# Two transfers at an image boundary: the fourth pair's spread reciprocals are issued two steps later

## The chip, the cores and the metric

The kernel runs on one core of a Trainium2 chip. The metric is the time of one execution in microseconds on the device; the lower the better. The core has five engines that run their own instruction streams: PE (matmuls; its weight loads are shown as PEld), DVE (vector), ACT (activations, casts; it also issues transfers), POOL (vector) and SP (issues most transfers). Each stream is in order. Engines and transfers wait for each other through counters (semaphores).

## The reference, cut to what matters

Two layers over a batch of 8 images of 384 channels and 32 x 32 = 1024 positions. The change lies in layer 0, an attention over the positions of one image with 8 heads of 48 channels and a relative bias:

```python
qkv = (tokens @ qkv_w + qkv_b).reshape(b, n, 3, NUM_HEADS, HEAD_DIM)
attn = jnp.einsum('bhnd,bhmd->bhnm', q * scale, k)
attn = attn + _relative_bias(h, w, mlp_w1, mlp_b1, mlp_w2, mlp_b2)[None]
attn = jax.nn.softmax(attn, axis=-1)
out = jnp.einsum('bhnm,bhmd->bhnd', attn, v)
out = out @ proj_w + proj_b
```

with `x + out` as its result, group norm ahead of it. Layer 1 is a second attention with 6 heads and a feed-forward part with quantised activations. All is float32.

## The kernel before, in words

Layer 0 goes image by image (`b` = 0 to 7). The 8 heads are held as four pairs (`pair` 0 to 3; the two heads of a pair, `j`, take 64 partitions each). The first three pairs carry 48 channels of their own and 16 channels of the fourth pair beside them; the fourth pair (`NF0` = 3) is put together from those by transfers between partitions.

*Units.* Per image there are 16 batches of four score units. `run` computes the scores of a batch (L920, tiles `s`), DVE adds the bias (L927), ACT takes the exponential (L931), and one batch later PE multiplies by `v` (L893). The row of ones in `v` gives the softmax sums, so `oT` holds the outputs not yet divided, and the sums beside them.

*Dividing.* When a pair is done, `divide` (named `divide` in the listing below) brings its sums to DRAM (L956) and back in another shape (L960), POOL takes reciprocals (L961), they go to DRAM (L967, `keep_inverse`), are loaded spread over 64 partitions for each of the two heads (L984, `spread`, tile `rb`, two loads of 256 KB), and POOL multiplies (L988, `multiply`). For the fourth pair `spread_rows` (L1000, `oT<-oT`, six transfers of 64 KB) then copies its rows to beside the first three pairs, because the output projection (`products`, L1011, tiles `pp`) reads three tiles with all 64 rows of both heads in use. `project_out` of image `b` is run inside image `b + 1`, after its first batch. It adds `res`, the image itself, loaded by SP (L1021).

*Between two images.* The next image's q and k are computed between its predecessor's last batch and its own first one, in six blocks (`BLOCKS0`; block 1 is the keys of pair 0, block 2 its queries, 3 the keys of pair 1, 4 its queries, 5 the keys of pair 2, 6 its queries). A block is three groups of products on PE (L171, `pm` and `pg`), one instruction on ACT (L677) and one on DVE (L683, `take` and `add`), and then `halves`: a cast on ACT to the high part (L696), a subtraction on DVE for the low part (L697), and transfers of both to DRAM: the high part is issued by ACT, the low one by SP (`halves<-h`, `halves<-t`; L701 is the whole tile of 512 KB, L703 two pieces of 64 KB). After block 3, PE computes `v` in four parts (`project_v`, L776). After v's second part `fill_q` and after the third `fill_k` issue the transfers that complete the first pair's queries and keys on chip (L719: `h<-t`, `km<-h`, `km<-l`, `h<-l`, `l<-h`, two each, ten in all, called fills here). Blocks 4 to 6 follow; then the new image's first batch, which reads the filled tiles, then `pp` of the old image, then the second batch.

*What sets the order.* A framework writes the waits. Beside it, the kernel puts off work by steps: `later.after(n, work)` runs `work` at the n-th `later.step()` from there. Between images, each block's `add` and each part of `v` is one step: blocks 1 to 3 are steps 1 to 3 after the last batch's `divide`, v's four parts are 4 to 7, blocks 4 to 6 are 8 to 10. A work's step sets its place in the streams of SP and POOL. The tuple `at` in `divide` holds such numbers: `at[0]` for `keep_inverse`, `at[1]` for `spread`, and from there `at[2]` for `multiply` and, for the fourth pair, from there `at[3]` for `spread_rows`.

*Transfer counters.* The framework gives the transfers of SP and ACT eight counters in turn, in the order in which it places them, and a transfer waits until the one that used its counter before has landed. Which two transfers are paired so is seen in the built program, not in the source.

The last image and the first three pairs take other branches of the same `if`.

Of the kernel before, what the change touches and what calls it, by code (L numbers as in the profile page):

```python
# [275 lines left out]
def _layer0(tc, ins, x1, sums, shared, weights, beside):  # L276
# [9 lines left out]
    with ExitStack() as ctx:  # L286
# [40 lines left out]
        for g in range(P // QT):  # L327
            at = g * QN
# [516 lines left out]
        def weigh(b, u, es):  # L845

            pair, h, m2 = u
            if m2 == 0:
                acc[b, pair] = mm2(f"o{b}_{pair}_{h}")
            po = acc[b, pair]  # L850
            for i in range(2):
                for r in range(2):
                    keys = ts(r, QP)
                    for j in range(2):
                        nc.tensor.matmul(  # L855
                            po[ts(j, S0), r], v[keys, 2 * m2 + i, 2 * pair + j, :],
                            es[j][keys, ts(i, HALF)], start=(m2 == 0 and i == 0),
                            stop=(m2 == MT // 2 - 1 and i == 1),
                        )
            if m2 < MT // 2 - 1:  # L860
                return None
            o = oT[:, pair, ts(h, HALF)]
            nc.scalar.copy(o, po[:, 0])

            def finish():
                nc.vector.tensor_add(o, po[:, 1], o)
                if h == NH - 1:
                    divide(b, pair)

            return finish  # L870
# [8 lines left out]
        class Batches:  # L879
# [7 lines left out]
            def weigh(self):  # L887
                pair, h, g, es = self.held
                self.held = None
                po = mm2(f"o{self.b}_{pair}_{h}_{g}")[:, 0]  # L890
                for i in range(BT):
                    for j in range(2):
                        nc.tensor.matmul(  # L893
                            po[ts(j, S0)], v[:, BT * g + i, 2 * pair + j, :],
                            es[i][:, ts(j, HALF)], start=(i == 0), stop=(i == BT - 1),
                        )

                def finish():
                    o = oT[:, pair, ts(h, HALF)]
                    if g == 0:  # L900
                        nc.scalar.copy(o, po)
                        return
                    nc.vector.tensor_add(o, po, o)  # L903
                    if h == NH - 1:
                        divide(self.b, pair)

                return finish
# [39 lines left out]
        def divide(b, pair):  # L947


            o = oT[:, pair]  # L950
            sd = dram.tile([2, N], F32, tag="sd", name=f"sd{b}_{pair}")
            rd = dram.tile([2, N], F32, tag="rd", name=f"rd{b}_{pair}")
            mine = sums[:, b, pair]
            inv = kept.tile([P, 2 * N // P], F32, tag="inv", name=f"inv{b}_{pair}", bufs=2)
            for j in range(2):
                nc.sync.dma_start(sd[j : j + 1], oT[j * S0 : j * S0 + 1, pair])  # L956

            def invert():
                with nc.allow_non_contiguous_dma(reason="sums"):
                    nc.sync.dma_start(mine, sd.rearrange("j (p c) -> (j p) c", c=2 * N // P))  # L960
                    nc.gpsimd.tensor_tensor(  # L961
                        inv, mine, over.to_broadcast([P, 2 * N // P]), ALU.pow
                    )

            def keep_inverse():
                with nc.allow_non_contiguous_dma(reason="sums"):
                    nc.sync.dma_start(rd.rearrange("j (p c) -> (j p) c", c=2 * N // P), inv)  # L967

            if b == B - 1 or b == 0 and pair < NF0:
                invert()  # L970
                at = (2, 2 if pair == NF0 else 3, 2, 0)
            elif pair == NF0:
                invert()
                at = 2, 5, 2, 1
            else:
                later.after(1, invert)
                at = 3, 4, 2, 0
            later.after(at[0], keep_inverse)
            rb = []

            def spread():
                rb.append(kept.tile([P, N], F32, tag="rb", name=f"rb{b}_{pair}"))
                for j in range(2):
                    nc.sync.dma_start(rb[0][ts(j, S0)], rd[j].partition_broadcast(S0))  # L984
                later.after(at[2], multiply)

            def multiply():
                nc.gpsimd.tensor_mul(o, o, rb[0])  # L988
                if b == B - 1:
                    if pair < NF0:  # L990
                        for j in range(2):
                            nc.gpsimd.memset(oT[j * S0 : j * S0 + SP, pair], 0.0)
                elif pair == NF0:
                    later.after(at[3], spread_rows)

            def spread_rows():
                for c in range(NF0):
                    for j in range(2):
                        row = j * S0 + SP + c * FR
                        nc.sync.dma_start(oT[j * S0 : j * S0 + SP, c], oT[row : row + FR, pair])  # L1000

            later.after(at[1], spread)
# [70 lines left out]
        for i in range(len(parts) // 2):  # L1073
            later.after(i + (13 if i < 9 else 12), lambda: grow_turns(1))
            at = 1 + i % NF0 if i < 12 else 2 + i % 2
# [1502 lines left out]
```

## Time and profile before

| | us |
|---|---|
| median of three runs | 2915.94 (2912.86 to 2917.39) |
| the profiled execution | 2915.22 |
| its span | 2913.4 |
| PE busy | 2872.4 (99%) |
| DVE busy | 2010.5 (69%) |
| ACT busy | 1554.4 (53%) |
| POOL busy | 492.7 (17%) |

Layer 0 takes the first 1340 us; the boundaries between its images lie 160 us apart, the first at about 230 us. In a line of the timeline or of the chain the first number is the start from the span's begin, the second the duration, then engine, line, operation and `output<-inputs`; an engine's name with q is its queue issuing a transfer. In brackets is the idle time of the engine ahead of the instruction, and what ended it. Times of landing are those of a transfer's last counter event in the trace. The windows view gives, for a stretch, the busy time of PE, PEld, DVE, ACT and POOL with the number of instructions, the granted clock of PE as a share of full speed, and the use of the transfer engines.

### The profile page before, as it was taken

Reading aid. Unit: us, or ns where it says so; the run is one execution under the profiler, and the core shown is the slowest. Engines: PE = TensorE matmul, PEld = TensorE weight load, DVE = VectorE, ACT = ScalarE, POOL = GpSimd, SP = SyncE. Lnnn points to the kernel's source line nnn. Section 1 sums busy time; section 2 is a strip of 40 time slices with the busy share of each in tenths; the row PEclk is TensorE's granted clock in tenths of the full one; section 3 lists DMA queues with packets and bytes.
Section 4 is the critical chain, followed back from the end, with each engine's and each line's share of the span. In section 5 each row is a group of like instructions: output and inputs, shape, how many; then the busy total and the mean of one; then the engine's idle time right before and its main releaser. Section 6 shows DMA issues by size and latency. Waiting matters only on the chain.

```text
span 2913.4 us, 43519 instructions
## 1 busy us (share of the span) xinstructions
PE 2872.4 (99%) x16850; PEld 1648.2 (57%) x16850; DVE 2010.5 (69%) x2041; ACT 1554.4 (53%) x1888; POOL 492.7 (17%) x318
## 2 busy tenths in 40 slices
PE   8999999999999999999999999999999999999998
PEld 3465564646464554644546647647647647655553
DVE  3886868686777768673756865865865875865756
ACT  2655636364555647362734655555555555564644
POOL 3120302121120202022102203203202202211010
PEclk9999999999999999999999999999999999999999
DMA  6657575665746474753301212112112112112111
GB/s 193 198 166 207 136 237 136 192 173 167 193 139 194 131 233 99 225 142 109 110 24 31 84 32 73 68 32 72 68 32 72 68 32 73 68 41 84 41 46 39
DMA packets 177751, 324.78 MB, mean 111 GB/s; under 512 B 75744, under 2 KB 94672, under 8 KB 176256
## 3 DMA queue, kind: packets, MB, share of 16 engines
q1 hardware_dynamic: 167552, 299.88, 36.1%
q10 hardware_dynamic: 9984, 22.02, 2.4%
q8 instruction: 137, 2.24, 0.3%
q14 instruction: 78, 0.64, 0.1%
HBM read 227.50 MB, written 80.65 MB: 106 GB/s over the span
## 4 chain that ended last, share of the span: by engine, by line
PE 86%; DMA 4%; DVE 4%; ACT 2%; issue 1%; SPq 1%; ACTq 0%; POOL 0%; DVEq 0%
PE o L893 14%; PE s L1930 11%; PE o L1979 11%; PE s L920 11%; PE y2p L2224 6%; PE pg L171 6%; PE y1p L2173 5%; PE pv L1867 4%; PE pm L171 3%; PE pp L2076 3%; PE pp L1011 3%; PE vg L776 2%; PE pq L1719 2%; PE s L824 1%; PE o L855 1%
## 5 line engine op out<-in xcount | busy, mean ns | idle before, releaser
L931 ACT ACTIVATE e<-e 128x1024 f32<-128x1024 f32 x448 | 473.9, 1058 | 324.9 <-DVE e L927 301.1
L927 DVE TENSOR_TENSOR e<-s,grow 128x1024 f32<-128x1024 f32 x448 | 517.4, 1215 | 86.6 <-PE s L920 79.8
L1941 ACT ACTIVATE e<-s,kc 128x512 f32<-128x512 f32 x768 | 464.0, 694 | 172.9 <-PE s L1930 163.3
L1930 PE MATMUL s<-qk,qk 64*64 64x512 f32 x3072 | 418.9, 592 | 1.7 <-DVE oT L1989 1.4
L1979 PE MATMUL o<-e,v 64*64 64x512 f32 x3072 | 414.5, 590 | 0.0
L893 PE MATMUL o<-e,v 128*64 128x512 f32 x1792 | 407.7, 598 | 1.3 <-DVE e L927 1.2
L1930 PEld LDWEIGHTS s<-qk,qk 64*64 64x64 f32 x3072 | 153.9, 132 | 191.9 <-issue 109.3
L1956 DVE TENSOR_TENSOR t<-t,e 128x1024 f32<-128x1024 f32 x192 | 230.9, 1221 | 45.2 <-ACT e L1941 45.0
L1979 PEld LDWEIGHTS o<-e,v 64*64 64x64 f32 x3072 | 160.6, 133 | 168.2 <-issue 141.1
L920 PE MATMUL s<-q,k 64*128 64x512 f32 x2016 | 254.0, 397 | 0.3 <-DVE oT L903 0.2
L893 PEld LDWEIGHTS o<-e,v 128*64 128x64 f32 x1792 | 120.5, 136 | 233.5 <-issue 217.2
L920 PEld LDWEIGHTS s<-q,k 64*128 64x128 f32 x2016 | 182.7, 184 | 104.2 <-DVE e L927 25.1
L961 POOL TENSOR_TENSOR inv<-sums,over 128x16 f32<-128x16 f32 x32 | 93.2, 2913 | 728.5 <-DMA sums<-sd 562.6
L2160 DVE TENSOR_REDUCE parts<-y 128x1 f32<-128x1024 f32 x75 | 89.7, 1217 | 103.2 <-ACT y L2157 102.7
L1953 DVE TENSOR_TENSOR t<-e,e 128x1024 f32<-128x1024 f32 x96 | 114.1, 1223 | 58.8 <-ACT e L1941 58.6
L1836 POOL TENSOR_TENSOR hc<-hc,rsqrt 128x32 f32<-128x32 f32 x24 | 137.9, 5747 | 2.0
L988 POOL TENSOR_TENSOR oT<-oT,rb 128x1024 f32<-128x1024 f32 x32 | 76.7, 2396 | 316.9 <-DMA rb<-rd 233.0
L1867 PE MATMUL pv<-wv,bx 128*128 128x384 f32 x384 | 128.3, 491 | 0.0
L2076 PE MATMUL pp<-oT,L_attn_proj_wT 128*128 128x512 f32 x288 | 126.3, 595 | 2.0 <-DVE oT L2042 2.0
L1011 PE MATMUL pp<-oT,wp 128*128 128x512 f32 x288 | 126.3, 596 | 1.0 <-issue 0.8
L1867 PEld LDWEIGHTS pv<-wv,bx 128*128 128x128 f32 x384 | 119.4, 314 | 9.8 <-ACT e L1941 4.1
L2173 PE MATMUL y1p<-lun,w 128*128 128x512 f32 x360 | 113.6, 396 | 2.8 <-DVE lun L2123 2.7
(242 smaller groups left out, 4256.2 us busy)
## 6 DMA issues: line engine op xcount, KB each, us to landing
rb<-rd SPq DMA_DIRECT2D x110, 256.0 KB
wc<-cut SPq DMA_DIRECT2D x42, 576.0 KB
k<-halves SPq DMA_DIRECT2D x84, 192.0 KB
wc<-there SPq DMA_DIRECT2D x25, 576.0 KB
halves<-h ACTq DMA_DIRECT2D x28, 512.0 KB
halves<-t SPq DMA_DIRECT2D x28, 512.0 KB
xn<-in_x_dram SPq DMA_DIRECT2D x24, 512.0 KB
res<-in_x_dram SPq DMA_DIRECT2D x24, 512.0 KB
```

What stands on the lines that cost most here:

```text
L171: self.nc.tensor.matmul(out[:, h], w[:, i, k], part[k][:, ts(h, HALF)], start=(k == 0 and i != 1), stop=(k == KC - 1 and i != 0),)
L893: nc.tensor.matmul(po[ts(j, S0)], v[:, BT * g + i, 2 * pair + j, :], es[i][:, ts(j, HALF)], start=(i == 0), stop=(i == BT - 1),)
L920: nc.tensor.matmul(ss[i][:, j], k[c][ts(j, S0), ts(BT * g + i, P)], q[a][ts(j, S0)], start=(m == 0), stop=(m == 2),)
L927: nc.vector.tensor_add(e.rearrange("p (j q) -> p j q", j=2), ss[i], near(2 * pair, BT * g + i, h, [GW * IW, 2]),)
L931: nc.scalar.activation(e, e, AF.Exp)
L1011: nc.tensor.matmul(pps[b, m][:, h], (wp[:, k] if k < NF0 else wl)[:, ts(m, P)], oT[:, k, ts(h, HALF)], start=(k == 0), stop=(k == (NF0 if ...
L1867: nc.tensor.matmul(pv[:, i, 0:C], xt[:, k].rearrange("c (p m) -> c m p", m=MT)[:, 2 * m2 + i], wv[:, k], start=(k == 0), stop=(k == KC - 1),)
L1930: nc.tensor.matmul(s[j][ts(c, QP), i], qk[pair, 1][rows, ts(4 * m2 + 2 * i + c, QP)], qk[pair, 0][rows, ts(h, HALF)], start=True, stop=True,)
L1941: nc.scalar.activation(e[:, ts(i, HALF)], s[j][:, i], AF.Exp, scale=kc[:, pair, j, m : m + 1])
L1956: nc.vector.tensor_add(total[j], total[j], e)
L1979: nc.tensor.matmul(po[ts(j, D1), r], v[keys, 2 * m2 + i, at : at + D1], es[j][keys, ts(i, HALF)], start=(m2 == 0 and i == 0), stop=(m2 == ...
L2173: nc.tensor.matmul(py[m][:, h], w1[:, k, ts(m, P)], un[k][i][:, ts(h, HALF)], start=(k == 0 and i == 0), stop=(k == KC - 1 and i == 1),)
```

## The change

For the fourth pair of every image but the last (`pair == NF0`, `b < B - 1`) `spread` is run at step 7 in place of 5, `multiply` one step later in place of two, and `spread_rows` one step after it as before. `keep_inverse` stays at step 2. In SP's stream the two `rb` loads move from ahead of the ten fills to behind them, and block 4's three `halves<-t` come ahead of the six `oT<-oT`. In POOL's stream the order of the instructions is the same. The matmuls and their order are the same.

```diff
             elif pair == NF0:
                 invert()
-                at = 2, 5, 2, 1
+                at = 2, 7, 1, 1
             else:
                 later.after(1, invert)
                 at = 3, 4, 2, 0
```

## The prediction

> **What bounds the kernel now.** I read the page first, then the waits of PE, then the chain at an image boundary, SP's queue there, and the windows view for the clock. The page says that PE is busy all the time, so only what takes time from PE counts.
>
> ```profile
> PE 2872.4 (99%) x16850; PEld 1648.2 (57%) x16850; DVE 2010.5 (69%) x2041; ACT 1554.4 (53%) x1888; POOL 492.7 (17%) x318
> ```
>
> PE's waits, longest in total first (engine, line, what it waited for: total, times, longest):
>
> ```profile
> PE s L920 <- DMA l<-h: 10.3, 6, 1.8
> ...
> PE s L920 <- DMA oT<-oT: 1.7, 1, 1.7
> ```
>
> The largest is at the seven boundaries between images of layer 0: the first scores of the new image wait for the last fill, `l<-h` (L719). The chain at the second boundary (start, us, what) shows why:
>
> ```profile
> 388.66 1.06 ACT h L696
> 389.72 0.02 issue
> 389.74 2.69 DMA halves<-h
> 392.43 0.02 issue
> 392.44 2.24 DMA l<-h
> 394.68 0.04 issue
> 394.73 4.37 PE s L920 x21
> 399.09 15.65 PE pp L1011 x36
> ```
>
> The fill is not late for its data: it is issued when ACT's copy `halves<-h` has landed. The built program hands out eight transfer counters in turn, and a transfer waits for the one that had its counter before; the built before pairs the last `l<-h` with ACT's copy of block 4. SP's queue at the same place:
>
> ```profile
> 377.06 1.26 SPq L984 DMA_DIRECT2D rb<-rd  x2
> 378.42 1.17 SPq L719 DMA_DIRECT2D h<-t  x2
> ...
> 385.21 7.74 SPq L719 DMA_DIRECT2D l<-h  x2
> 393.05 5.60 SPq L1000 DMA_DIRECT2D oT<-oT  x6
> 398.75 0.52 SPq L701 DMA_DIRECT2D halves<-t  x1
> ```
>
> The windows view (last fields: granted clock, DMA share, GB/s), second and third boundary:
>
> ```profile
> 386.00:419.00 33.00, 31.29 (x120) 17.62 (x120) 17.33 (x15) 10.58 (x11) 0.29 (x1) 0.95 0.72 222
> 549.00:581.00 32.00, 30.05 (x120) 16.37 (x120) 17.67 (x15) 10.40 (x10) 0.00 (x0) 1.00 0.73 217
> ```
>
> A clock of 0.95 over 33 us is 1.65 us lost, that is 3.3 us at half speed; the trace has it as 3.4 us at 0.5. It happens at boundaries 2, 4 and 6, right after the stall, and nowhere else before the last instructions. PE starts a pair of score products every 0.43 us there, against 0.23 us in later batches.
>
> **The change part by part.**
>
> *Work.* No instruction is added or removed; the two `rb` loads (256 KB each), the POOL multiply and six `oT<-oT` move. Per image SP issues the ten fills first, then `rb`, then block 4's three `halves<-t`, then `oT<-oT`.
>
> *The fills.* In before, `rb` lies ahead of them in the transfers: in the trace's landing events `rb` lands at 382.70 and 383.72 and the first fills at 384.0. In the built after each fill is paired with an earlier transfer of SP, ACT's copy of block 3 or the weights, all landed by 381. Issued one after the other at 0.6 us (1.17 us for two), with two waits of about 2.2 us (`l<-h`'s 2.24), the last lands at about 385. PE needs it at 392.3, so this stall goes at all seven boundaries, with 7 us to spare.
>
> *`rb` and the multiply.* `rb` is issued at about 383.4. Before, two loads took 377.06 to 383.72 in a full queue; so it lands between 387 and 390. The multiply (2.41 us, 383.88 before) ends by 389.8 to 392.4. Nothing else on POOL waits for it; only `oT<-oT` does.
>
> *What is late next.* The projection `pp` (L1011) needs `oT<-oT`: the first two for its first matmul. In after the first `oT<-oT` has the counter of ACT's big copy of block 5 (`halves<-h`, L701); in before it had block 4's, and only the fifth waited for block 5's. So `pp` now hangs on this chain of ACT:
> - cast of block 4 (L696): before at 388.66, waiting for PE. Its buffer is now one that the fills free, so it starts when ACT's L677 ends, 385.39 + 1.12 = 386.5: 2.13 us earlier.
> - its three copies, issued in 1.6 us, the last landing 2.53 us after its issue (393.13 before): 391.0 + d, where d is what contention adds.
> - cast of block 5, which waits for them: 393.20 before, 391.07 + d after. PE and DVE feed it by 390.7.
> - its big copy: 1.07 + 2.69 us (the row above, undisturbed): 394.83 + d.
> - two `oT<-oT`: 0.6 us to the second issue, 2.41 us to its landing (393.63 to 396.04 before), 0.1 us of hand-overs: `pp` at 397.9 + d, that is 4.73 us + d after the start that the cast of block 5 had in before.
>
> In before `pp` started 4.70, 5.82, 4.75, 5.89, 4.65, 5.43 and 4.64 us after that cast at the seven boundaries; at 5 and 6 it then waited 0.71 and 0.44 us more for `oT<-oT` (its matmuls at 886.60 and 1047.32), which the new spacing avoids. The gains before d are -0.03, 1.09, 0.02, 1.16, 0.63, 1.14 and -0.09: 3.9 us. Boundaries 1 and 7 further lose about 0.35 us each in before, where the second batch waits for `res` (landing 252.15, PE's next stage at 254.77); `res` is issued about 1 us earlier in after, so 0.7 us more: 4.6 us.
>
> *d.* Now SP's `halves<-t` of block 4 (512 KB, issued at about 388.9) runs beside ACT's copies. Bounds: 0 (the 2.53 us, alone), and 3.0 us: ACT's copies of block 3, issued at 371.77 and 372.40 beside SP's loads, landed at 376.51 and 377.88, 5.5 us for the last. Nearer is ACT's copy at 395.16 beside `oT<-oT`, 3.42 us, d = 0.9; but only the end of ACT's transfer meets SP's here, so I take d = 0.3. 7 x 0.3 = 2.1: the gain is 2.5 us.
>
> [...]
>
> *The clock.* Without the stall PE goes through the four score units at 0.23 us a pair, up to the fourth, which waits for DVE's first addition (1.23 us after L697's 1.23 us after the cast of block 5): it ends at about 395.7 + d. Then PE waits for `pp`, until 397.9 + d: 2.2 us idle, as long as the 2.1 us that it waits in before (392.6 to 394.73). In before three of seven such gaps were followed by 3.4 us at half clock. In `pp`, where one matmul follows another at 0.43 us, that costs 3.4 x 0.5 = 1.7 us. Bounds: none of seven (0) and all (11.9 us). I take three, as before: 5.1 us. What the gate cost in before is already in the gains of boundaries 2, 4 and 6.
>
> [...]
>
> *Sum.* -2.5 + 5.1 = +2.6 us, 0.09%. The profiled execution took 2915.22 us (span 2913.4), 0.72 below the median 2915.94. On the median: 2918.5 us.
>
> **The rivals.** What a measurement can tell from no change is about 0.2%, 5.8 us.
>
> *A: `pp` does not wait (faster).* If `oT<-oT` landed by the time PE reaches `pp`, the gain would be the stall and the slow clock: `pp` at about 395.9 instead of 399.0 at even boundaries, at 558.4 instead of 560.4 at odd ones: 3 x 3.1 + 4 x 2.0 = 17 us, 2899. For: `rb` and the multiply are early enough. Against: the counter of ACT's copy of block 5, which cannot land before 394.8. It decides if that copy were 1.9 us faster, which no row shows. Half of it, with no slow clock, would be 2907.
>
> *B: the slow clock falls into `pp` at most boundaries (slower).* Place: `pp` on PE. Price 1.7 us each. From five of seven on the loss passes 5.8 us (5 x 1.7 - 2.5 = 6.0); at seven 9.4, 2925. For: the gap is slightly longer, and a short wait of about 0.5 us before the fourth unit precedes it. Against: three of seven in before.
>
> *C: the change does not do what it says.* The fills stay behind a late transfer: no change, 2916. The pairing in the built after speaks against it.
>
> **How the numbers follow.** My case and all between 4.6 us faster (d = 0, no slow clock) and 5.8 slower: 0.56. A and what lies towards it: 0.12. B, or d near 1: 0.30. C: 0.02. So faster 0.12, same 0.58, slower 0.30. Range: the low end 2910 is the 4.6 us gain and a little of A; the high end 2926 is B with seven of seven; a tenth is left out on each side.
>
> **What would show it.** Right: no wait of PE for `l<-h`; `rb` behind the fills in SP's queue; ACT's cast of block 4 about 2 us earlier; PE waiting 1.5 to 2.5 us for `oT<-oT` ahead of `pp` seven times; windows at the boundaries with a clock under 1 at two to four places, now in `pp`. Wrong: `pp` following the scores without a wait (A); the clock under 1 at five or more, or not at all; ACT's copies of block 4 landing over 3 us after their issue (d too small).

## The result, and the profile after

The changed kernel takes 2937.38 us (median of four runs, 2933.4 to 2940.08) against 2916.66 us before (four runs, 2912.86 to 2918.36): the ratio is 1.0075, with a 95% interval of 1.0063 to 1.0087. It is 20.7 us slower. The prediction was 2918.5 us, range 2910 to 2926: the measured time lies outside, on the side of rival B. All four runs of the changed kernel have a granted clock of 0.993 over the span (the profiled run before: 0.998), so the half clock told of below is not that of one execution alone.

The page of the profile after (span 2933.8 us), engines' busy time:

```profile
PE 2878.7 (98%) x16850; PEld 1649.3 (56%) x16850; DVE 2010.2 (69%) x2041; ACT 1553.3 (53%) x1888; POOL 497.0 (17%) x318
```

PE has the same instructions and is busy 6.3 us longer; the other 14 us of the longer span (20.4) are idle time. Its two largest waits (what it waited for: total, times, longest) are at the image boundaries, and the wait for `l<-h` is gone, as it should be:

```profile
PE pp L1011 <- DVE e L927: 17.2, 7, 2.5
PE s L920 <- DVE e L927: 11.0, 7, 2.1
```

Before, the stall was 1.7 us at each of the seven boundaries, 12.0 us in all (the view puts the 1.7 us of the fourth down to `oT<-oT`). So 12.0 us of waiting went and 28.2 us came, at the same seven places. The first of the two lines is the wait ahead of `pp`, the second the wait ahead of the fourth score unit of the first batch, which PE starts when DVE has added the bias to the first. The group of `pp`'s products (busy us, mean ns of one | idle before) shows the third loss, in after and, behind it, in before:

```profile
L1011 PE MATMUL pp<-oT,wp 128*128 128x512 f32 x288 | 139.6, 647 | 17.2 <-DVE e L927 17.2
```

```profile
L1011 PE MATMUL pp<-oT,wp 128*128 128x512 f32 x288 | 126.3, 596 | 1.0 <-issue 0.8
```

The same 288 products take 13.3 us longer: PE's clock. (PE's whole busy time grows by less, because the first batch's scores, into which the half clock fell before, are shorter now: at the second boundary one pair of products follows another every 0.23 us where it was 0.43.) The windows view of after (last fields: granted clock, share of the transfer engines, GB/s), three of the seven boundaries:

```profile
386.00:421.00 35.00, 30.93 (x110) 17.59 (x110) 15.31 (x13) 9.38 (x9) 2.40 (x1) 0.95 0.74 218
550.00:587.00 37.00, 32.71 (x113) 18.56 (x113) 15.00 (x13) 9.70 (x10) 2.40 (x1) 0.91 0.75 218
714.00:752.00 38.00, 34.05 (x123) 20.21 (x123) 16.68 (x16) 10.49 (x10) 2.41 (x1) 0.96 0.76 216
```

Before, three of seven boundaries had a clock under 1; now all seven do. In the trace's clock record that is 34.1 us at half speed around the boundaries instead of 10.2.

From a boundary's first score to the end of the last product of `pp` it is 153.2 us in seven boundaries before and 175.4 after. Of the 22.1 us more, 9.0 lie ahead of `pp`'s first product and 13.1 within `pp`; about 1.7 us come back elsewhere (the span grew by 20.4). The chain at the second boundary (start, us, what) shows how `pp` becomes late:

```profile
389.30 1.04 ACT h L696
...
391.21 4.34 DMA halves<-h
...
395.65 1.06 ACT h L696
396.71 0.02 issue
396.74 1.23 DVE t L697
397.96 1.14 DVE e L927
399.10 1.13 DVE t L683
400.23 0.06 DVE e L927
400.29 0.99 issue
401.27 1.23 DVE e L927
402.50 0.04 issue
402.55 17.37 PE pp L1011 x36
```

The last of ACT's copies of block 4 takes 4.34 us from issue to landing (before: 2.53), so the cast of block 5 starts 6.36 us after that of block 4 (before: 4.54, 393.20 less 388.66), and with it everything that follows. ACT's stream before, at the same place:

```profile
390.12 1.24 ACTq L703 DMA_DIRECT2D halves<-h  x2
...
393.20 1.04 ACT L696 CAST h<-t 128x1024 fp32r<-128x1024 f32 x1 [0.62 <-DMA halves<-h]
```

The last steps of the chain after are a trap: the view puts `pp`'s wait down to DVE's addition L927, since it ended last (402.49). But the second `oT<-oT` landed at 402.41, and at all seven boundaries `pp` begins 0.14 to 0.25 us after that landing. Experiment e5 decides it. SP's queue at that place, and what it waited for:

```profile
387.05 1.22 SPq L719 DMA_DIRECT2D l<-h  x2
388.32 1.23 SPq L984 DMA_DIRECT2D rb<-rd  x2
391.61 0.34 SPq L701 DMA_DIRECT2D halves<-t  x1
392.00 2.10 SPq L703 DMA_DIRECT2D halves<-t  x2
399.49 3.71 SPq L1000 DMA_DIRECT2D oT<-oT  x6
```

```profile
SPq L1000 <- DMA halves<-h: 5.3, 1, 5.3
```

The multiply ended at 395.56, yet `oT<-oT` was issued at 399.49, 0.06 us after ACT's big copy of block 5 landed (399.43), whose counter it has; SP had nothing else to issue in between. At the other six boundaries it is 0.06 to 0.08 us. Right beside ACT's copies of block 4 (issued 390.36 to 391.21) SP now has `rb` (landing 393.00) and `halves<-t` (issued 391.61, landing 395.72).

### The profile page after: what moved, and what is told of

Read it like the earlier page. It is cut to its first block, busy times and chain, and to the rows that moved or that the text cites. A ratio compares the mean times of both kernels' runs of the same rounds, so it can differ in the third digit from the quotient of the medians.

```text
span 2933.8 us, 43516 instructions
## 1 busy us (share of the span) xinstructions
PE 2878.7 (98%) x16850; PEld 1649.3 (56%) x16850; DVE 2010.2 (69%) x2041; ACT 1553.3 (53%) x1888; POOL 497.0 (17%) x318
## 4 chain that ended last, share of the span: by engine, by line
PE 86%; DVE 5%; DMA 4%; ACT 3%; issue 2%; SPq 0%; ACTq 0%; POOL 0%; DVEq 0%
PE o L893 13%; PE s L1930 11%; PE o L1979 11%; PE s L920 10%; PE y2p L2224 6%; PE pp L1011 5%; PE y1p L2173 5%; PE pg L171 4%; PE pv L1867 4%; PE pp L2076 3%; PE pm L171 3%; PE s L824 2%; PE o L855 2%; PE pq L1719 2%; PE vg L776 1%
## 5 line engine op out<-in xcount | busy, mean ns | idle before, releaser
L927 DVE TENSOR_TENSOR e<-s,grow 128x1024 f32<-128x1024 f32 x448 | 517.6, 1216 | 87.7 <-PE s L920 82.9
L1930 PEld LDWEIGHTS s<-qk,qk 64*64 64x64 f32 x3072 | 153.9, 132 | 190.6 <-issue 109.8
L1011 PE MATMUL pp<-oT,wp 128*128 128x512 f32 x288 | 139.6, 647 | 17.2 <-DVE e L927 17.2
```

The lines of the kernel that those rows point to most:

```text
L927: nc.vector.tensor_add(e.rearrange("p (j q) -> p j q", j=2), ss[i], near(2 * pair, BT * g + i, h, [GW * IW, 2]),)
L1011: nc.tensor.matmul(pps[b, m][:, h], (wp[:, k] if k < NF0 else wl)[:, ts(m, P)], oT[:, k, ts(h, HALF)], start=(k == 0), stop=(k == (NF0 if ...
L1930: nc.tensor.matmul(s[j][ts(c, QP), i], qk[pair, 1][rows, ts(4 * m2 + 2 * i + c, QP)], qk[pair, 0][rows, ts(h, HALF)], start=True, stop=True,)
```

## The experiments

Three theories were set against each other. **P** (place): the counter of ACT's copy of block 5 holds `oT<-oT` back and makes `pp` late. **T** (transfers): SP's transfers beside ACT's copies of block 4 delay the cast of block 5. **G** (gate): PE's clock is halved after the gaps (34.1 us of it in after), and that is a loss of its own. X stands for the start of the cast of block 5. The cuts of e1 and e2 are against before, that of e6 is against e2 (also called rb_only), those of e3, e4 and e5 (after_pool) are against after, and that of e7 (pool_late) is against e5.

**e1, only the later half of the change**

```diff
-                at = 2, 5, 2, 1
+                at = 2, 5, 3, 1
```

> Only the later half of the change: rb is loaded ahead of the fills as before, but the multiply and the six oT<-oT come a step later, so that they stand behind block 4's halves<-t and carry the counter of ACT's copy of block 5. Before 2916.7 us, after 2937.4 us. Theory P (the place of oT<-oT makes the projection late): pp starts 6.9 us after the cast of block 5 (as after) instead of 4.6 to 5.8 (before), 12 us in seven boundaries, the wait for l<-h stays, and the half clock follows into pp at most boundaries (up to 13 us more): 2929 to 2941 us. Theory T (rb's transfers beside ACT's copies of block 4 are what costs): without them the copies land in 2.5 us again and the cast of block 5 is where it was: at most 2922 us. Theory G (the clock gate is most of the loss): whatever the place, the time follows the number of windows at half clock, 1.7 to 3.4 us each; with three of them the time stays under 2930 us.

Measured: 2950.66 us, ratio 1.0106 (1.009 to 1.0123). The chain at the second boundary:

```profile
396.72 2.51 DMA halves<-h
...
399.30 1.05 ACT h L696
400.35 0.02 issue
400.37 4.77 DMA halves<-h
405.14 0.02 issue
405.16 2.26 DMA oT<-oT
407.42 0.14 issue
407.55 18.39 PE pp L1011 x36
```

ACT's copies of block 4 take 2.5 us again, so T's part is absent, and still it is the slowest of these variants of `at`: P holds, beyond the range that was given for it. Here the second `oT<-oT` has the counter of block 5's copy, which now runs beside block 4's `halves<-t` and takes 4.77 us, so `pp` comes 8.2 us after X instead of 6.9. All seven boundaries have the half clock, 51.2 us in all.

**e2, only the first half of the change**

```diff
-                at = 2, 5, 2, 1
+                at = 2, 7, 0, 1
...
-                later.after(at[2], multiply)
+                if at[2]:
+                    later.after(at[2], multiply)
+                else:
+                    multiply()
```

> Only the first half of the change: rb is loaded behind the fills, the multiply is issued in the same step, and oT<-oT keep the step that they had before, ahead of block 4's halves<-t and with counters of landed fills. Theory P: pp no longer waits, it starts about 0.8 us after the last scores (about 4.7 us after the cast of block 5 instead of 6.9), 15 us less than after, and without that gap no half clock in pp, 13 us less: about 2909 us, faster than before. Theory T: rb still runs beside ACT's copies of block 4, which take 3.4 to 4.6 us, and the fourth score unit still waits 2 to 2.7 us for DVE: 2918 to 2930 us. Theory G: the gap ahead of the fourth score unit is as long as the one of before, which was followed by the half clock three times in seven: 5 us on top, about 2914 us.

Measured: 2916.27 us against 2917.5 before, ratio 0.9999 (0.9989 to 1.0009): no difference. Waits of PE, and of SP at the second boundary:

```profile
PE s L920 <- DVE res L1030: 6.1, 9, 1.1
PE pp L1014 <- DMA oT<-oT: 4.1, 5, 1.2
```

```profile
SPq L703 <- DMA halves<-h: 6.1, 1, 6.1
```

Moving `rb` alone costs nothing: the 20 us of the change come with the order of `oT<-oT` and block 4's `halves<-t` (P). That order is behind T too. Here `rb` still runs beside ACT's copies of block 4, but `halves<-t` come later, and the copies land 2.4 to 3.3 us after the last issue, not the 3.4 to 4.6 that T had for `rb`; the distance of the two casts is 1.8 us above that of the prediction's chain (4.57 us) in seven boundaries, where after has 12.2. `pp` starts 4.7 to 5.6 us after X, and no boundary is followed by the half clock. But the removed wait for `l<-h` brings nothing either. SP now waits 6.1 us for ACT's copy of block 6, by another such pair of counters, ahead of block 5's parts and `res`; the second batch's scores then wait for `res`. Theory P's 2909 us had left out that next wait.

**e3, PE kept busy while it waits for `oT<-oT`** (after, with three products more, which the first real product overwrites)

```diff
                 pps[b, m] = mm2(f"pp{b}_{m}")
+                if m == 0 and pairs[0] == 0 and b < B - 1:
+                    for _ in range(3):
+                        nc.tensor.matmul(
+                            pps[b, 0][:, 0, :C], wp[:, 0, :P], wp[:, 1], start=True, stop=True
+                        )
```

> The kernel after with three more matmuls (128 x 384, own weights, about 1.9 us together) into pp's accumulator ahead of its first product, which overwrites them. PE is then busy in most of the 3.0 us in which it waits for oT<-oT; pp's start doesn't move. Theory G: the half clock at the boundaries goes or gets rarer, and pp takes 14.7 us again instead of 16.2 to 17.8: 8 to 13 us less than after, 2924 to 2929 us. Theory P and T without the clock: the loss is the late start alone, and nothing is gained: 2937 us. If it is the gap ahead of the fourth score unit that sets the gate, the windows stay too.

Measured: 2929.29 us, ratio 1.0037 (1.0026 to 1.0047). That is 8 us less than after by the medians and 11 by the two ratios, and PE has more to do. The chain at the second boundary, and the group of `pp`'s real products:

```profile
394.77 1.06 ACT h L696
...
399.40 2.20 PE pp L1011 x6
401.60 0.07 issue
401.67 15.69 PE pp L1016 x36
```

```profile
L1016 PE MATMUL pp<-oT,wp 128*128 128x512 f32 x288 | 125.2, 593 | 0.2
```

At this boundary `pp` starts 6.9 us after X as in after (401.67 less 394.77), and its 288 products take 125.2 us in all instead of 139.6. G holds: the half clock is a loss beside the late start. Of the windows at half clock 13.7 us are left, one at each of the last four boundaries. They fall mostly into the added products, and `pp` starts 8.0 to 8.4 us after X there, which takes back some 5 us of the gain. The gap ahead of the fourth score unit is still there at all seven (15.0 us of waiting in all).

**e4, the projection after the second batch**

```diff
-                if i == 1 and b > 0:
+                if i == 3 and b > 0:
```

> The kernel after with the output projection of the image before issued after the second batch of the new image instead of the first, so that the scores of the second batch lie under the wait for oT<-oT. Theory P: the wait of pp (3.0 us, seven times) goes, and with it the half clock in pp: about 21 us and up to 13 us less than after, minus what the second batch then waits for ACT and DVE; 2905 to 2916 us. Theory T: the gap ahead of the fourth score unit (2.0 to 2.7 us) stays, since block 5's cast is as late: not under 2915 us. Theory G: if that one gap still brings the half clock, it falls into scores that are limited by ACT or DVE, and costs less than in pp.

Measured: 2956.37 us, ratio 1.0131 (1.0115 to 1.0148): 40 us above what P had, and none of the three theories had forecast a loss against after. PE's waits:

```profile
PE o L893 <- DVE e L927: 25.6, 10, 3.5
PE s L920 <- DVE e L927: 15.4, 25, 3.8
```

`pp` no longer waits for `oT<-oT`. But `pp` had been the work under which DVE and ACT made the first batch's exponentials; without it PE waits for these in the second batch, 3.5 us at a time, and the half clock (37.5 us) follows those gaps instead.

**e5, `oT<-oT` taken off the shared counters** (after, with the six transfers issued by POOL)

```diff
-                        nc.sync.dma_start(oT[j * S0 : j * S0 + SP, c], oT[row : row + FR, pair])
+                        nc.gpsimd.dma_start(oT[j * S0 : j * S0 + SP, c], oT[row : row + FR, pair])
```

> The kernel after with the six oT<-oT issued by POOL, right behind its multiply, instead of SP. They then hold none of the eight counters that SP and ACT share, and wait for the multiply alone (it ends at 395.6 us at the second boundary); everything else stays in its order. Theory P (it is the counter of ACT's copy of block 5 that holds oT<-oT back): they are issued 2 to 4 us earlier, pp starts about 0.8 us after the last scores instead of 3.0, and without that gap the half clock in pp goes: 15 + 13 us less than after, 2909 to 2915 us, about as before. Rival (SP's queue or the multiply makes oT<-oT late, not the counter): they still land at X + 6.8 us (X = cast of block 5) and the time stays at about 2937 us. Theory T: the gap of 2 to 2.7 us ahead of the fourth score unit stays in both cases, since rb and SP's halves<-t still run beside ACT's copies; if half the windows at half clock stay with it, about 2918 us.

Measured: 2913.33 us, ratio 0.9994 (0.9983 to 1.0005): 24 us less than after, as before. POOL's stream, the chain behind the cast of block 5, and PE's largest wait:

```profile
391.69 2.39 POOL L988 TENSOR_TENSOR oT<-oT,rb 128x1024 f32<-128x1024 f32 x1 [25.21 <-DMA rb<-rd]
394.38 3.02 POOL L1000 DMA_DIRECT2D oT<-oT  x6 [0.30 <-POOL oT L988]
```

```profile
394.36 1.06 ACT h L696
...
397.86 0.98 PE s L920 x6
398.84 0.20 issue
399.04 15.69 PE pp L1011 x36
```

```profile
PE s L920 <- DVE e L927: 12.5, 7, 3.3
```

The transfers go out 0.3 us after the multiply. `pp` starts 4.7 us after X, ahead of DVE's third addition (399.99 to 401.20; its counterpart in after ended at 402.49), so it was not that addition that it had waited for in after. The run takes `oT<-oT` off SP's stream and off its counter at once; that it was the counter is seen in after, where SP had issued all that stood ahead by 394.10, the multiply had ended at 395.56, and the wait of 5.3 us ended with ACT's copy at all seven boundaries. Together they settle P. The gap ahead of the fourth score unit stays, as T says, and three boundaries (1, 4 and 6) still have the half clock, 13.7 us in all.

**e6, rb_only with `res` earlier**

```diff
+                if n == len(BLOCKS0) - 1:
+                    place = shared.weights(f"res{b}")
+                    res = residuals(b, lambda name, place=place: place[:, ts(int(name[-1]), N)])
                 if held_halves is not None:
                     held_halves()
...
-            place = shared.weights(f"res{b}")
-            res = residuals(b, lambda name, place=place: place[:, ts(int(name[-1]), N)])
```

> The rb_only kernel (rb behind the fills, oT<-oT where they were) with the three loads of res issued ahead of block 5's halves<-t instead of behind them. In rb_only the first scores of the second batch wait for res at every boundary (0.6 to 1.4 us beyond the usual spacing, about 7 us in all), which is where the gain of the removed wait for l<-h went: SP waits 6 us for ACT's copy of block 6 before block 5's parts and res. Theory: res lands 1.5 to 2 us earlier, these waits go, 5 to 7 us less than rb_only: about 2910 us, faster than both kernels. Rival: res is late for the counter of ACT's copy of block 6 alone, in front of which the move doesn't bring it, and the time stays at 2916 us.

Measured: 2910.09 us (12 runs) against 2916.85 (23 runs), ratio 0.998 (0.997 to 0.999): faster than both kernels. The waits for `res` are gone from PE's list. The largest that are left at the boundaries are

```profile
PE pp L1014 <- DMA oT<-oT: 3.3, 4, 1.1
PE s L920 <- DVE e L927: 1.8, 2, 1.6
PE pp L1014 <- DVE e L927: 1.3, 1, 1.3
```

The second and third of these lie at the first boundary (1.57 and 1.32 us), the only one with the half clock (6.8 us) in the profiled execution, which took 2914.65 us, more than the median.

So about half of the removed `l<-h` wait of 12 us is gained, 6 to 7 us, once the three transfers behind it (`oT<-oT`, `halves<-t`, `res`) have places where little waits for them.

**e7, block 4's `halves<-t` later** (after_pool, and)

```diff
-                    for queue, x, part in ((nc.scalar, 0, up), (nc.sync, 1, down)):
...
+                    move_out(nc.scalar, 0, up)
+                    if n == BB:
+                        later.after(2, lambda: move_out(nc.sync, 1, down))
+                    else:
+                        move_out(nc.sync, 1, down)
```

(`move_out` holds the old loop's body.)

> The after_pool kernel (oT<-oT issued by POOL), with SP's three halves<-t of block 4 issued two steps later, behind block 5's, so that only rb is left beside ACT's copies of block 4. Theory T in the form that the runs so far leave (it is mostly the 512 KB of halves<-t, not rb, that stretches ACT's copies from 2.5 to 3.4 to 4.7 us after their last issue): they land within 3.1 us again, the cast of block 5 comes 1 to 1.5 us earlier, and the gap ahead of the fourth score unit (12.5 us in seven boundaries) shrinks to 4 us or less: 6 to 9 us less than after_pool, about 2906 us. Rival (rb stretches them, or the gap is set by DVE's own order): copies and gap as in after_pool, 2913 us.

Measured: 2916.16 us, ratio 0.9995 (0.9984 to 1.0006). PE's waits:

```profile
PE pp L1017 <- DMA oT<-oT: 11.9, 8, 3.7
...
PE s L926 <- DVE e L933: 2.7, 4, 1.1
```

The mechanism was right and the time wrong. The gap ahead of the fourth score unit falls from 12.5 to 2.7 us, and ACT's copies of block 4 land 2.3 to 3.6 us after the last issue, where after_pool had 3.5 to 6.0: T holds, and `halves<-t` is the larger part of it, as in e2: the distance of the two casts is 3.3 us above the 4.57 in seven boundaries here, and 13.7 in after_pool. What is left has `rb` still beside the copies. But block 5's `halves<-t` have moved up too (first issue 2.3 us after X at the second boundary, against 5.3 in after_pool) and run beside `oT<-oT`, the second of which takes 4.74 us there (3.08 in after_pool), and `pp` waits 11.9 us for them, with the half clock at three boundaries: what was gained in one gap is lost in the next.

**e8, the same with `res` and the multiply earlier** (`at = 2, 7, 0, 1` as in e2, and e6's edit)

> The same, with rb's multiply in rb's own step and the loads of res ahead of block 5's halves<-t. In after_pool nothing waits for res, so the theory expects no more from it than from pool_late, about 2906 us; if res's 1.5 MB, now issued earlier, run beside ACT's copies of block 5 and 6, nothing that PE waits for hangs on these, and the time should be the same within 2 us.

Measured: 2941.0 us, ratio 1.0073 (1.0057 to 1.0089): a clear miss.

```profile
PE pp L1020 <- DMA oT<-oT: 31.1, 8, 5.5
```

`res` (three loads of 512 KB) now runs beside `oT<-oT` as well: at the second boundary the loads are issued from 396.19 and land at 400.79 to 407.77, and the second `oT<-oT`, issued at 397.46, lands 7.8 us later, where e7 had 4.74. All seven boundaries have the half clock again (34.1 us). The run moves the multiply as well, and does not try the two apart; but the lateness lies behind the issue of `oT<-oT`, not ahead of it. It had been expected that nothing PE waits for hangs on these transfers; `oT<-oT` themselves do.

## Why the prediction was wrong, step by step

*The fills and the stall: right.* No wait for `l<-h` is left. The last fill lands at 389.99, 5.2 us ahead of the first score at 395.17 (7 were said).

*`rb` and the multiply: late, by a little more than the bounds.* At this boundary everything stands 2.88 us later than before (ACT's L677 of block 5 starts at 388.27 instead of 385.39). So shifted, `rb` was expected by 392.9 and the multiply's end between 392.7 and 395.3; they came at 393.00 and 395.56. The step "`rb` is issued at about 383.4" failed by 2 us: SP took 8.65 us for the ten fills (379.67 to 388.32) where the sum had 6.3. Two of them (383.08, 384.53) went out only as the transfers that had their counters landed (383.06, 384.51), and two took 1.3 us to issue instead of 0.6.

*What is late next: right in kind and in its chain.* Cast of block 4 was said for 389.4 with this shift, and came at 389.29. From there every later member is late by nearly the same amount: the cast of block 5 by 1.70 us against the chain with d = 0 (395.65 against 393.95), `pp`'s first product by 1.77 (402.55 against 400.78). That amount is d.

*d: this is the term that was mis-sized.* The step "only the end of ACT's transfer meets SP's here, so I take d = 0.3" is wrong. From the two casts (their distance less the 4.57 us of the chain with d = 0), d is 0.90, 1.79, 2.04, 1.64, 1.38, 2.10 and 2.31 us at the seven boundaries, 12.2 us in all where 2.1 were taken. It lies inside the bounds of 0 to 3.0, and the row that was set aside as too far (copies of block 3 beside SP's loads, d = 3.0) was as near as the one chosen. With `rb` 2 us later, 512 KB of `rb` and 512 KB of `halves<-t` meet the copies over nearly their whole length; e2 and e7 show that `halves<-t` is most of it. Not only the end of ACT's transfers was stretched: the 512 KB copy, the first of the three, took 3.78 us from issue to landing (390.36 to 394.14) where before's took 2.69.

*The clock: rival B, and dearer than B.* The step "I take three, as before" failed: it was seven of seven, and three of the seven windows last 6.8 us instead of 3.4. At full clock `pp` takes 15.69 us (e3, e5), 109.8 in seven boundaries; in after it takes 123.9. So the price within `pp` was 14.1 us where 5.1 were taken. The reason given for three was that the new gap of 2.2 us is "as long as the 2.1 us that it waits in before". That compared unlike things: the 2.1 run from the start of the last product ahead of the stall (392.62), the 2.2 from the end of the last score. From end to start, as the waits view counts, the gap was 1.7 us before and 2.4 to 2.5 us after, at all seven boundaries. The "short wait of about 0.5 us" before the fourth unit was 1.6 on average (11.0 in seven), since it hangs on the late cast. e3 gave 8 to 11 us of the time back by keeping PE busy.

*The sum with the measured terms.* -4.6 (the prediction's gain without d and without the clock) + 12.2 (d) + 14.1 (clock) = +21.7 us; the span grew by 20.4 and the median by 20.7. The frame of the sum held to about 1 us, and two of its terms did not. (Of the -4.6, the 0.44 us at boundary 6 were read as a wait for `oT<-oT`, but were the half clock: its window ran from 1043.9 to 1047.3, and the two transfers that this product needs had landed by 1043.89.) The two terms were also not independent: d lengthens one gap, and in e5, which leaves that gap alone, three boundaries still have the half clock. The range was built from B with seven windows at d = 0.3 (2925) and left out both bounds together, 7 x 3.0 for d and 11.9 for the clock, which would have reached to about 2944.

*Rival A.* It hung on the counter of block 5's copy, as the prediction said; with that counter out of the way (e5) `pp` does follow the scores, 0.2 us after their end. Even so the time is only that of before: 12.5 us in the gap ahead of the fourth unit and 13.7 us of half clock stand where before had 12.0 us of the stall and 10.2 of half clock.

## What to carry to other kernels

Where a framework hands out a few transfer counters in turn, moving a transfer also changes which unrelated transfer it waits for (here ACT's copy of block 5, 5.3 us of SP's time at the second boundary): read the pairs from the built program, for the moved transfers and for those behind them, and where a pair is bad, take the transfer off the shared counters or put it where its partner has long landed. Between two stages that are full of transfers, a wait that is removed is worth only what the next three in line leave of it (6 to 7 of 12 us in e6). When two unknown terms feed each other (here a contention that made a gap 1.6 us long on average, and the half clock, which followed at seven boundaries in place of three), the range needs both at their bad ends together. And two gaps are compared in one measure, both from the end of the last product.

## What the runs showed of the hardware

*The windows at half clock.* In the clock records of before and after each window at half clock, but for the one at the end of the span, lasts 3.413 us or, three times in after, 6.827. The starts within one trace lie whole multiples of 3.413 us apart: 395.3, 719.6 and 1043.9 us before are 95 of these apart, 402.5 and 566.4 us after are 48. The gap of 1.7 us was followed by the half clock at three of the seven boundaries in before (2, 4 and 6); the gaps of 2.4 to 2.5 us in after, each with a shorter one close ahead of it (1.6 us on average), at seven of seven. Keeping PE busy in them (e3) took the half clock from 34.1 us to 13.7. Why the gap of 1.7 us was not followed by it at the other four boundaries is not shown: no run varied the length or the place of a gap alone.

*Transfers of two queues at once.* ACT's three copies (640 KB) land 2.5 us after the last issue when alone (e1 at 396.72, and before) and 3.4 to 4.7 us beside SP's `rb` and `halves<-t` (after).

*Six small transfers issued by POOL* took it 3.0 us of issue (e5, 394.38), where SP took 3.71 us (after).
